# Layer 2 of a fused four-layer graph network: one 512-column moving operand, edge counts on ScalarE, another sequence

## The chip, the cores and the metric

One core of a Trainium2 chip runs one kernel launch that computes all four layers for all 16 graphs. The metric is the device time of that launch in microseconds. An engine is named as in the profile: PE is TensorE (its matmuls; PEld are its weight loads), DVE is VectorE, ACT is ScalarE, POOL is GpSimd, SP is SyncE, which here only issues transfers.

## The reference

Each of 16 graphs has 1024 nodes with 256 features and a symmetric 0/1 adjacency with self-loops. Every layer is x = x + f(relu(layernorm(x)), adj). Layers 0 and 1 are single-head attention layers, layer 3 is a four-head attention layer with a layer norm of its own, and layer 2, which the change is about, is a mean over neighbours:

```python
def _L2_gnn_ref(x, adj, W_msg, W_upd, bias):
    a = adj.astype(x.dtype)
    h = jnp.einsum('bnf,fu->bnu', x, W_msg)
    msg_sum = jnp.einsum('bij,biu->bju', a, h)
    deg = jnp.sum(a, axis=1)
    messages = jnp.where(deg[..., None] > 0, msg_sum / jnp.maximum(deg, 1.0)[..., None], 0.0)
    out = jnp.einsum('bnf,fu->bnu', x, W_upd) + messages + bias
    return jax.nn.relu(out)
...
x = x + _L0_gnn_ref(h, adj, L0_gnn_W, L0_gnn_a)      # attention over axis 1, elu
x = x + _L1_gnn_ref(h, adj, L1_gnn_W, L1_gnn_a)      # attention over the last axis, elu
x = x + _L2_gnn_ref(h, adj, L2_gnn_W_msg, L2_gnn_W_upd, L2_gnn_bias)
x = x + _L3_gnn_ref(h, adj, L3_gnn_W, ...)           # 4 heads of 64
```

## The kernel before

Nodes lie on the 128 partitions, eight tiles of 128 nodes to a graph. `graph(b)` writes out the four layers of graph b as a generator that yields now and then; a loop at the end of `tile_simple_stack` interleaves the generators of neighbouring graphs by the numbers they yield, so that the first layer of graph b+1 lies beside the last ones of graph b. That gives a rank to each instruction. The class `Order` then schedules everything anew: it walks through time with a planned cost for each instruction (`costs`), takes on each engine the ready instruction of the lowest rank, and fixes the order that comes out by dependencies. `STAY` says how far in rank it may deviate in order to stay in layer 3's half-array matmuls (128x64 weights, line 1238) or out of them, because PE pays for the change between the two kinds. So each number in a `yield`, in `STAY`, `APART`, `LEAD` or `SHIFT` moves instructions on all engines.

The matmuls are in fp32, except in layer 2. There, line 1154 projects a node tile with the message weights into PSUM. ScalarE writes the scaled result twice: `hi` in fp32r, a shorter format (line 1156), and `rest` in fp32 (line 1158); DVE stores the difference as `lo`, also fp32r (line 1159). `hi` and `lo` are the two parts of the messages. The 0/1 adjacency comes as eight column blocks of 512 KB through POOL's queue (`load_adj`, line 828), four buffers in turn. For each block j of 128 receiving nodes, PE multiplies the block with the eight tiles of `hi` and then with the eight tiles of `lo`, 258 columns each (line 1170), into the bank that already holds the update projection (line 1164). Columns 256 and 257 of `hi` are 1 and 0, so that column 256 of the sum counts the edges; `lo` has zeros there. ScalarE scales the result into `v` (line 1178) and copies the count into `edges` (line 1179), DVE adds the bias (line 1180), and `residual` adds the result to x and begins the next layer's norm. The PSUM pool `hd_ps` (two banks) holds the results of layer 2 and of layer 3's heads.

Elsewhere: line 936 are the projections of all layers, 930 the transposes of the normed input, 1040 and 1102 the products of layers 0 and 1 with their weights `p`, which DVE makes (lines 1048, 1050 and 1109); line 1225 makes the weights of a head of layer 3, and line 1246 is ScalarE's copy of a head's result out of PSUM. `Mask.step` (line 820) turns the adjacency into bytes and sums the edges by ScalarE. `tail` is the norm at the end of layer 3. At the very end DVE compares the edges of `squares` with those of `edges`, and a flag decides whether a slower general version runs after it.

Of the kernel before, what the change touches and what calls it, by code (L numbers as in the profile page):

```python
# [9 lines left out]
F32 = mybir.dt.float32  # L10
# [5 lines left out]
P = 128  # L16
# [405 lines left out]
class Order:  # L422
# [7 lines left out]
    STAY = {False: 31470.0, True: 35569.0}  # L430
# [33 lines left out]
    def costs(self, k):  # L464
# [182 lines left out]
def tile_simple_stack(  # L647
# [46 lines left out]
    unread = const.tile([P, D], U8)  # L694
    ones = const.tile([P, P], F32)
# [136 lines left out]
    def inv_std(var, n, scale, eps):  # L832

        rs = tile_of(small, [P, NT * H], F32, tag="rstd", name="rs", bufs=6)
# [7 lines left out]
    class Norm:  # L842
# [22 lines left out]
        def pair(self, xs, g, sums=None):  # L865
# [16 lines left out]
            if sums is not None:  # L882
                for k in range(2):
                    nc.scalar.activation(  # L884
                        unread, xs[:, 2 * g + k, :], AF.Square, bias=shift[:, k : k + 1], accum_out=self.var[:, 2 * g + k : 2 * g + k + 1]
# [78 lines left out]
    class Row:  # L964
# [5 lines left out]
        def add(self, n, f):  # L970
# [3 lines left out]
            nc.tensor.matmul(self.ps[g][:, k * P : (k + 1) * P], ones, diag, start=True, stop=True)  # L974
# [36 lines left out]
    def layer0(b, xs, m, norm, after):  # L1011
# [8 lines left out]
        for n in range(NT):  # L1020
# [5 lines left out]
            yield 3.85  # L1026
# [5 lines left out]
        yield 5.25  # L1032
# [11 lines left out]
        for j in range(NT):  # L1044
# [14 lines left out]
            yield 2.21  # L1059
        for i, ps in enumerate(early):  # L1060
            product(ps, i, NT - 1)
        for i in range(NT):
# [11 lines left out]
            yield 3.49  # L1074


    def layer1(b, xs, mask, norm, after):
        hs = new_hs()
        by_pe = Row() if b == 0 else None
        for n in range(NT):  # L1080
# [4 lines left out]
            yield 0.77  # L1085
# [9 lines left out]
        yield 2.71  # L1095
# [10 lines left out]
        for j in range(NT):  # L1106
# [6 lines left out]
            yield 3.18  # L1113
        for i in range(NT):
# [14 lines left out]
            yield 4.42  # L1129
# [9 lines left out]
    def layer2(b, xs, norm, after):  # L1139
# [8 lines left out]
        hi = tile_of(state, [P, NT, W3], F32R, tag="hs", name="hi", bufs=3)  # L1148
        lo = tile_of(state, [P, NT, W3], F32R, tag="hs", name="lo", bufs=3)
        nc.vector.memset(hi[:, :, D : D + 1].bitcast(F32), 1.0)  # L1150
        nc.vector.memset(hi[:, :, D + 1 : D + 2].bitcast(F32), 0.0)
        nc.vector.memset(lo[:, :, D : D + 2].bitcast(F32), 0.0)
        for n in range(NT):
            ps = project(norm, wx[2], n, D)
            by = z[:, n : n + 1]
            nc.scalar.activation(hi[:, n, :D], ps[:, :D], AF.Copy, scale=by)  # L1156
            rest = tile_of(work, [P, D], F32, tag="e", name="rest", bufs=2)
            nc.scalar.activation(rest, ps[:, :D], AF.Copy, scale=by)
            nc.vector.tensor_tensor(lo[:, n, :D], rest, hi[:, n, :D].bitcast(F32), op=OP.subtract)
            yield 0.91  # L1160
        for j in range(NT):
# [6 lines left out]
            for h in (hi, lo):  # L1168
                for i in range(NT):
                    nc.tensor.matmul(  # L1170
                        ps[:, : D + 2], adj_n[j][:, i, :], h[:, i, : D + 2],
                        start=False, stop=(h is lo and i == NT - 1), skip_group_check=True,
                    )
            k = b * NT + j
            if j + 4 < NE:
# [3 lines left out]
            nc.scalar.copy(edges[:, k : k + 1], ps[:, D : D + 1])  # L1179
            nc.vector.tensor_tensor(v, v, rows["bias2"], op=OP.add)  # L1180
            residual(xs, j, v, after)
            yield 1.61


    def layer3(b, xs, mask, norm, res):
# [6 lines left out]
        for n in range(NT):  # L1192
# [12 lines left out]
            yield 1.07  # L1205
# [11 lines left out]
        yield 3.57  # L1217
        for h in range(H):
            next_row = everywhere(d_row[h + 1], "row3") if h + 1 < H else None
            pss = [tile_of(hd_ps, [P, HALF], F32, tag="hd", name="ps_o3", bufs=2) for _ in range(NHALF)]  # L1220
            for j in range(0, NT, run):
# [21 lines left out]
                yield 1.17 * run  # L1243
# [6 lines left out]
    def tail(b, xs, hs, res):  # L1250
# [4 lines left out]
        for g in range(NHALF):  # L1255
# [7 lines left out]
            yield 20.37  # L1263
            nc.vector.tensor_tensor(of, of, hs[:, t, :D].rearrange("p t (h e) -> p t h e", e=HO), op=OP.add)
            yield 4.99
            nc.vector.tensor_reduce(m[:, 0, :], o, axis=AX.X, op=OP.add)
            yield 3.22
            total = m[:, 0, :].unsqueeze(2).to_broadcast([P, PER * H, HO])
            nc.vector.scalar_tensor_tensor(o, total, -1.0 / HO, o, op0=OP.mult, op1=OP.add)
            yield 8.10  # L1270
# [8 lines left out]
        for t, o, of, m, sq in halves:  # L1279
            nc.vector.tensor_reduce(m[:, 1, :], sq, axis=AX.X, op=OP.add)  # L1280
            rs.append(inv_std(m[:, 1, :], PER * H, 1.0 / HO, 1e-6))
            yield 1.47
        for g, (t, o, of, m, sq) in enumerate(halves):
            r = rs[g][:, : PER * H].unsqueeze(2).to_broadcast([P, PER * H, HO])
            if g == 0:

                nc.vector.tensor_tensor(of, of, along("gamma3"), op=OP.mult)
                yield 10.12
                of1 = halves[1][2]
                nc.vector.tensor_tensor(of1, of1, along("gamma3"), op=OP.mult)  # L1290
                yield 0.66
            nc.vector.tensor_tensor(o, o, r, op=OP.mult)
            yield 0.00
            if b < B - 1:
                nc.vector.tensor_tensor(of, of, along("beta3"), op=OP.add)
            yield 5.43
# [4 lines left out]
            yield 0.82  # L1301

    def graph(b):
# [5 lines left out]
        for g in range(NT // 2):  # L1309
            norm.pair(xs, g)  # L1310
            m.step()
            yield 2.74
        for layer, inputs in ((layer0, (m,)), (layer1, (m.bytes,)), (layer2, ())):
            yield 1.81
# [5 lines left out]
        yield 1.19  # L1320
# [7 lines left out]
    def loads(b):  # L1328
        loaded[b] = load_x(b)
        yield 17.93  # L1330
        masks[b] = Mask(b)
        yield 0.17


    APART, LEAD = 129.59, 35.70
    SHIFT = {0: 3.07, 1: 1.51, 2: 0.13, 13: -0.44, 14: -0.27, 15: -0.26}
    def more():

        weights01(1, w1, w1_t, a1, (1, 0))
        yield 89.77  # L1340
        weights2()
        yield 0.34
        weights3()
        yield 27.01
# [6 lines left out]
    queue = [(58, 0, more())] + [(begins[b], b, graph(b)) for b in range(B)] + [(begins[b] - LEAD, b, loads(b)) for b in range(1, B)]  # L1351
# [10 lines left out]
    bad = tile_of(small, [P, 4], F32, tag="bad", name="bad", bufs=4)  # L1362
# [79 lines left out]
```

## Time and profile before

| | |
|---|---|
| time, median of 3 runs | 2426.45 us (2425.6 to 2430.18) |
| the profiled execution's own time | 2429.41 us |
| its span | 2428.0 us |
| mean granted TensorE clock | 0.991 |
| instructions | 63180, of which 26244 matmuls and as many weight loads |

The span is the stretch from the first to the last recorded instruction, and the execution's time is 1.4 us longer. In the profile, "mean ns" of a matmul is the time in the pipeline of one, from its start to its modelled end. Matmuls overlap, so the rate at which PE takes them is read from the chain of work, where a row gives the stretch of time that so many of them fill one after the other. An fp32 matmul of the program appears as two in the trace, an fp32r matmul and a transpose as one.

### The profile page before, as it was taken

To read this page: it belongs to the slowest core of one execution; us is meant where nothing else is said; L and a number is where in the kernel's file an instruction comes from. 1 tells how busy PE (TensorE), PEld (TensorE's weight loads), DVE (VectorE), ACT (ScalarE), POOL (GpSimd) and SP (SyncE) were. 2 spreads that over 40 slices of the span, in tenths; PEclk is the share of its full clock that TensorE was granted. 3 is DMA by queue.
4 is the path that set the end of the run, shared out by engine and by line. 5 is a ranking of instruction groups with operands and counts; after the bars stand their busy time and mean duration, and the time that the engine had idled before them with its cause. 6 is when DMAs were issued, how large, how long until landed. Compare 5 with 4: busy or idle time off the path is not lost.

```text
span 2428.0 us, 63180 instructions
## 1 busy us (share of the span) xinstructions
PE 2361.5 (97%) x26244; PEld 2106.7 (87%) x26244; DVE 1964.4 (81%) x3871; ACT 1455.2 (60%) x4062; POOL 469.3 (19%) x454
## 2 busy tenths in 40 slices
PE   7999999999999999999999999999999999999984
PEld 5889888988888889888998989889888998989874
DVE  6478697996979888787897969879787896978867
ACT  5765657567475665757567475665757566475340
POOL 1120310303113031220303113031220303103021
PEclk9999999999999999999999999999999999999997
DMA  5452342624344263342624334263342634244021
GB/s 177 88 110 89 70 97 87 140 85 92 94 105 101 84 126 98 79 97 78 142 93 92 93 101 106 84 119 101 84 97 75 144 93 92 89 104 89 19 63 37
DMA packets 212008, 231.65 MB, mean 95 GB/s; under 512 B 10328, under 2 KB 160960, under 8 KB 211712
## 3 DMA queue, kind: packets, MB, share of 16 engines
q0 software_dynamic: 137728, 83.90, 19.5%
q1 hardware_dynamic: 73984, 143.62, 18.9%
q8 instruction: 208, 3.41, 0.6%
q14 instruction: 88, 0.72, 0.1%
HBM read 210.25 MB, written 17.22 MB: 94 GB/s over the span
## 4 chain that ended last, share of the span: by engine, by line
PE 86%; DMA 5%; ACT 4%; DVE 3%; POOL 1%; issue 1%; SPq 0%; ACTq 0%; DVEq 0%
PE ps_o L1238 18%; PE ps_o L1040 17%; PE ps_proj L936 17%; PE ps_o L1102 16%; PE ps_o L1170 10%; PE ps_o L1164 4%; PE pt_h L930 4%; DMA raw<-in_adj_t 4%; ACT mask L820 1%; DVE p L1225 1%; POOL rs L836 1%; ACT hn L911 1%; ACT hi L1156 1%; DMA d_row<-e_row 0%; DMA row<-d_row 0%
## 5 line engine op out<-in xcount | busy, mean ns | idle before, releaser
L1225 DVE SCALAR_TENSOR_TENSOR p<-row,q,mask 128x1024 f32<-128x1024 f32 x512 | 617.9, 1279 | 63.0 <-PE ps_o L1238 58.6
L936 PE MATMUL ps_proj<-wx,ht 128*128 128x258 f32 (+2 forms) x2048 | 514.3, 387 | 6.7 <-ACT hs L1194 3.9
L1238 PEld LDWEIGHTS ps_o<-hb,p 128*64 128x64 f32 x16384 | 488.1, 138 | 27.8 <-issue 20.6
L1238 PE MATMUL ps_o<-hb,p 128*64 128x65 f32 x16384 | 502.2, 223 | 4.7 <-DVE p L1225 2.3
L1040 PE MATMUL ps_o<-hs,p 128*128 128x256 f32 x2048 | 477.8, 381 | 4.3 <-ACT hs L1052 4.3
L1102 PE MATMUL ps_o<-hs,p 128*128 128x257 f32 x2048 | 468.8, 382 | 3.9 <-ACT v L1127 2.2
L1102 PEld LDWEIGHTS ps_o<-hs,p 128*128 128x128 f32 x2048 | 381.5, 190 | 61.4 <-ACT v L1127 6.9
L936 PEld LDWEIGHTS ps_proj<-wx,ht 128*128 128x128 f32 x2048 | 371.7, 191 | 67.6 <-ACT hs L1082 6.5
L1040 PEld LDWEIGHTS ps_o<-hs,p 128*128 128x128 f32 x2048 | 381.1, 191 | 54.8 <-ACT hs L1052 4.7
L835 POOL TENSOR_SCALAR rs<-mv 128x4 f32<-128x4 f32 (+1 forms) x112 | 44.9, 401 | 1317.6 <-ACT unread L884 1298.9
L836 POOL TENSOR_TENSOR rs<-rs,neg_half 128x4 f32<-128x4 f32 (+2 forms) x144 | 265.9, 1846 | 12.0
L911 ACT ACTIVATE hn<-xs,shift 128x256 f32<-128x256 f32 x384 | 177.1, 504 | 77.3 <-PE pt_h L930 43.0
L1170 PE MATMUL ps_o<-hi,adj 128*128 128x258 f32 x1024 | 202.3, 320 | 2.1 <-ACT hi L1156 1.0
L1246 ACT ACTIVATE res<-ps_o 128x260 f32<-128x260 f32 x128 | 49.8, 389 | 254.2 <-PE ps_o L1238 253.9
L820 ACT ACTIVATE mask<-raw 128x512 uint8<-128x512 int32 x248 | 156.1, 632 | 53.6 <-DMA raw<-in_adj_t 52.7
L930 PE MATMUL pt_h<-ident,hn 128*128 128x128 f32 x1024 | 175.8, 278 | 2.0 <-ACT hn L911 1.8
L1006 DVE SCALAR_TENSOR_TENSOR xs<-v,xs 128x256 f32<-128x256 f32 x384 | 160.3, 418 | 17.8 <-ACT v L1127 11.2
L828 POOL DMA_DIRECT2D adj<-in_adj x128 | 114.8, 899 | 293.9 <-PE ps_o L1170 292.3
L1170 PEld LDWEIGHTS ps_o<-hi,adj 128*128 128x128 f32 x1024 | 150.1, 190 | 14.9 <-ACT hi L1156 5.4
L1048 DVE SCALAR_TENSOR_TENSOR p<-row,q 128x1024 f32<-128x1024 f32 x128 | 161.4, 1271 | 1.8 <-ACT row L980 1.6
L930 PEld LDWEIGHTS pt_h<-ident,hn 128*128 128x128 f32 x1024 | 126.0, 141 | 36.5 <-ACT hn L911 10.3
L931 ACT COPY ht<-pt_h 128x512 f32<-128x512 f32 x256 | 147.1, 575 | 16.8 <-PE pt_h L930 14.0
(124 smaller groups left out, 3009.0 us busy)
## 6 DMA issues: line engine op xcount, KB each, us to landing
raw<-in_adj_t SPq DMA_DIRECT2D x256, 256.0 KB
adj<-in_adj POOLq DMA_DIRECT2D x128, 512.0 KB, 5.3
row<-d_row SPq DMA_DIRECT2D x108, 512.0 KB
xs<-in_x POOLq DMA_DIRECT2D x32, 512.0 KB, 4.4
out<-xs SPq DMA_DIRECT2D x32, 512.0 KB
wx<-in_w SPq DMA_DIRECT2D x3, 256.0 KB
d_row<-e_row SPq DMA_DIRECT2D x45, 4.0 KB
wts<-in_w_t SPq DMA_DIRECT2D x2, 256.0 KB
```

Of the source, the lines that this page charges most:

```text
L820: nc.scalar.activation(to, raw, AF.Square, accum_out=total)
L836: nc.gpsimd.tensor_tensor(rs[:, :n], rs[:, :n], neg_half[:, :n], op=OP.pow)
L911: nc.scalar.activation(hn, xs[:, 2 * g + k, :], AF.Relu, scale=scale, bias=bias)
L930: nc.tensor.transpose(pt[:, c, k * P : (k + 1) * P], hn[:, c * P : (c + 1) * P], ident)
L936: nc.tensor.matmul(ps[:, :width], norm.ht[:, c, n * P : (n + 1) * P], w[:, c, :width], start=(c == 0), stop=(c == DC - 1))
L1006: nc.vector.scalar_tensor_tensor(x, v, 0.0, x, op0=OP.max, op1=OP.add, accum_out=after.sums[:, i % 2 : i % 2 + 1])
L1040: nc.tensor.matmul(ps[:, :D], ps_[j][:, i * P : (i + 1) * P], hs[:, j, :D], start=(j == 0), stop=(j == NT - 1))
L1048: nc.vector.scalar_tensor_tensor(p, row_a, q[:, j : j + 1], row_b, op0=OP.mult, op1=OP.max)
L1102: nc.tensor.matmul(ps[:, : D + 1], ps_[j][:, i * P : (i + 1) * P], hs[:, j, : D + 1], start=(j == 0), stop=(j == NT - 1))
L1170: nc.tensor.matmul(ps[:, : D + 2], adj_n[j][:, i, :], h[:, i, : D + 2], start=False, stop=(h is lo and i == NT - 1), skip_group_check=True,)
L1225: nc.vector.scalar_tensor_tensor(p, row, q[:, jj, h : h + 1], mask[:, jj, :], op0=OP.max, op1=OP.mult)
L1238: nc.tensor.matmul(pss[g][part, k * HW : (k + 1) * HW], ps_[t][:, i * P : (i + 1) * P][:, part], hbv[:, j + t, h, :], start=(j == 0 and t ...
```

## The change

In layer 2, `hi` and `lo` of a node tile lie side by side in one tile of 512 columns, and PE multiplies an adjacency tile with both at once, into the whole bank: eight matmuls of 512 columns for each block j instead of sixteen of 258. The two parts are no longer summed by the accumulation in PSUM: ScalarE scales the left half as before, and a new DVE instruction scales the right half and adds it. The column of ones is gone, and with it ScalarE's small copy; instead ScalarE reads each adjacency block (1024 numbers to a partition) in a copy that nobody reads and takes its sum. The sums now go by rows rather than by columns of the adjacency, so the comparison at the end is made on the totals of each graph. Three small memsets to a graph go. The planned cost of an fp32r matmul gets a term for its size. All numbers that lay the sequence are new, so the schedule as a whole is another one.

```diff
-    STAY = {False: 31470.0, True: 35569.0}
+    STAY = {False: 70844.0, True: 16885.0}
...
             if any("float32r" in a[3] for a in acc):
-                return 121.0, 330.0
+                t = max(121.0, 3.0 + size[0] / 2.4)
+                return t, t + 210.0
...
-    unread = const.tile([P, D], U8)
-    ones = const.tile([P, P], F32)
+    unread = const.tile([P, N], U8)
+    ones = const.tile([P, 1], F32)
...
-        hi = tile_of(state, [P, NT, W3], F32R, tag="hs", name="hi", bufs=3)
-        lo = tile_of(state, [P, NT, W3], F32R, tag="hs", name="lo", bufs=3)
-        nc.vector.memset(hi[:, :, D : D + 1].bitcast(F32), 1.0)
-        nc.vector.memset(hi[:, :, D + 1 : D + 2].bitcast(F32), 0.0)
-        nc.vector.memset(lo[:, :, D : D + 2].bitcast(F32), 0.0)
+        both = [tile_of(state, [P, NT, W3], F32R, tag="hs", name="hl", bufs=3) for _ in range(NHALF)]
+        hl = []
         for n in range(NT):
+            g, k = divmod(n, PER)
+            hl.append(both[g].rearrange("p n d -> p (n d)")[:, k * HALF : (k + 1) * HALF])
+            hi, lo = hl[n][:, :D], hl[n][:, D:]
             ps = project(norm, wx[2], n, D)
             by = z[:, n : n + 1]
-            nc.scalar.activation(hi[:, n, :D], ps[:, :D], AF.Copy, scale=by)
+            nc.scalar.activation(hi, ps[:, :D], AF.Copy, scale=by)
             rest = tile_of(work, [P, D], F32, tag="e", name="rest", bufs=2)
             nc.scalar.activation(rest, ps[:, :D], AF.Copy, scale=by)
-            nc.vector.tensor_tensor(lo[:, n, :D], rest, hi[:, n, :D].bitcast(F32), op=OP.subtract)
-            yield 0.91
+            nc.vector.tensor_tensor(lo, rest, hi.bitcast(F32), op=OP.subtract)
+            yield 0.77
...
-            for h in (hi, lo):
-                for i in range(NT):
-                    nc.tensor.matmul(
-                        ps[:, : D + 2], adj_n[j][:, i, :], h[:, i, : D + 2],
-                        start=False, stop=(h is lo and i == NT - 1), skip_group_check=True,
-                    )
+            for i in range(NT):
+                nc.tensor.matmul(ps, adj_n[j][:, i, :], hl[i], start=False, stop=(i == NT - 1), skip_group_check=True)
             k = b * NT + j
+            nc.scalar.activation(
+                unread, adj_n[j].rearrange("p i c -> p (i c)").bitcast(F32), AF.Copy, accum_out=edges[:, k : k + 1]
+            )
             if j + 4 < NE:
                 adj_n.append(load_adj(b, j + 4))
             v = tile_of(work, [P, D], F32, tag="v", name="v", bufs=2)
             nc.scalar.activation(v, ps[:, :D], AF.Copy, scale=z[:, j : j + 1])
-            nc.scalar.copy(edges[:, k : k + 1], ps[:, D : D + 1])
+            nc.vector.scalar_tensor_tensor(v, ps[:, D:], z[:, j : j + 1], v, op0=OP.mult, op1=OP.add)
             nc.vector.tensor_tensor(v, v, rows["bias2"], op=OP.add)
             residual(xs, j, v, after)
-            yield 1.61
+            yield 1.94
...
-                yield 1.17 * run
+                yield 2.07 * run
...
-    APART, LEAD = 129.59, 35.70
+    APART, LEAD = 146.48, 41.63
...
-    nc.vector.tensor_tensor(t, t, edges, op=OP.not_equal)
-    nc.vector.tensor_reduce(bad[:, 0:1], t, axis=AX.X, op=OP.add)
-    nc.vector.tensor_scalar(t, edges, 0.0, None, op0=OP.is_le)
+    t_0 = tile_of(work, [P, D], F32, tag="v", name="t_0", bufs=2)[:, : B * NT]
+    nc.vector.tensor_scalar(t_0, t, 0.0, None, op0=OP.is_le)
+    nc.vector.tensor_reduce(bad[:, 0:1], t_0, axis=AX.X, op=OP.add)
+    nc.vector.tensor_tensor(t, t, edges, op=OP.subtract)
+    nc.vector.tensor_reduce(bad[:, 3:], t.rearrange("p (b n) -> p b n", b=B), axis=AX.X, op=OP.add)
...
```

The other yields, `SHIFT`, and the sizes of a few small tiles change as well.

More of the change, by code (lines that the diff above doesn't have):

```diff
@@ L973, in add @@
             nc.vector.tensor_scalar(diag, ident, f, None, op0=OP.mult)
[L974 removed]
+            nc.tensor.matmul(self.ps[g][:, k * P : (k + 1) * P], ones.to_broadcast([P, P]), diag, start=True, stop=True)
         def rows(self, scales, tag="row"):
@@ L1350, in tile_simple_stack @@
     begins = [b * APART + SHIFT.get(b, 0.0) for b in range(B)]
-    queue = [(58, 0, more())] + [(begins[b], b, graph(b)) for b in range(B)] + [(begins[b] - LEAD, b, loads(b)) for b in range(1, B)]
+    queue = [(106.61, 0, more())] + [(begins[b], b, graph(b)) for b in range(B)] + [(begins[b] - LEAD, b, loads(b)) for b in range(1, B)]
     while queue:
```

78 lines of the change are left out of this document (39 added, 39 removed).

## The prediction

> **What bounds the kernel now.** I read the page's totals first, then the steady stretch by windows, then the chain in order of time, then the groups and waits of layer 2.
>
> ```profile
> span 2428.0 us, 63180 instructions
> PE 2361.5 (97%) x26244; PEld 2106.7 (87%) x26244; DVE 1964.4 (81%) x3871; ACT 1455.2 (60%) x4062; POOL 469.3 (19%) x454
> ```
> PE is busy nearly always. As its ends are modelled, that alone does not make it the bound, so I look at stretches: one whole steady graph (1044 to 1190), its layer 2 (1141.7 to 1178), and the end.
>
> ```profile
> 1044.00:1190.00 146.00, 145.65 (x1637) 130.73 (x1636) 121.56 (x238) 90.98 (x255) 29.39 (x28) 1.00 0.40 99
> 1141.70:1178.00 36.30, 36.21 (x233) 33.16 (x232) 25.27 (x64) 25.63 (x74) 13.58 (x13) 1.00 0.53 110
> 1164.00:1178.00 14.00, 14.00 (x99) 13.31 (x98) 13.91 (x34) 8.65 (x25) 9.00 (x8) 1.00 0.43 79
> 2320.00:2428.00 108.00, 67.77 (x1220) 61.24 (x1218) 82.07 (x115) 24.41 (x70) 26.06 (x16) 0.83 0.23 56
> ```
> The columns are the stretch, its length, busy PE, PEld, DVE, ACT and POOL, then clock, DMA share and GB/s. In a steady graph PE leaves 0.35 us of 146; DVE has 24 us and ACT 55 us left. In layer 2's second part DVE is nearly full too (13.91 of 14). At the end, where no next graph fills the holes, PE is not the bound.
>
> ```profile
> 148.38 1.92 PE ps_o L1170 x16
> 133.68 1.96 PE ps_o L1170 x16
> 165.47 1.73 PE ps_o L1040 x8
> 387.41 17.60 PE ps_o L1102 x80
> 2139.50 17.60 PE ps_o L1102 x80
> ```
> These rows of the chain (start, us, what) give rates: 16 fp32r matmuls of 258 columns fill 1.92 to 1.96 us, 120 to 122.5 ns each; eight fp32 ones of 256 columns 1.73 us, 216 ns each. The last two rows show the period: the same piece of layer 1 recurs twelve graphs later, so (2139.50 - 387.41) / 12 = 146.0 us for a graph. Period times number of graphs is what the kernel's time is made of, and the period is PE's work.
>
> **The change part by part. Matmuls.** A graph has 8 x 16 = 128 matmuls of 258 columns, 128 x 0.121 = 15.5 us. It gets 64 of 512. No row shows an fp32r matmul of 512 columns. The dear end is growth in proportion: 0.121 x 512 / 258 = 240 ns, 15.4 us for 64, a gain of 0.1 us. For the cheap end I take the half-array rows of layer 3, where 256 matmuls of 65 columns fill 7.62 us, two at a time: 59.5 ns for a pair. From there to 216 ns at 256 columns an fp32 column costs 0.82 ns and the fixed part is 6 ns. An fp32 matmul of 256 columns thus occupies PE as long as 512 fp32r columns at half that price would: 0.41 x 512 + 6 = 216 ns. By the same formula 258 columns would cost 112 ns; the 8 to 10 ns above it look like something that a short matmul does not cover, such as its weight load, and in the rows of 216 ns a weight load of the same 128 columns is covered. I take 216 ns, as the row of L1040 is nearest: it has the same weights and the same time at PE. That makes 64 x 0.216 = 13.8 us, a gain of 1.7 us for a graph; if the 8 ns stay, 64 x 0.224 = 14.3, a gain of 1.2. Over 16 graphs: 27 us, with 19 and 2 as the worse ends.
>
> [...]
>
> **ScalarE.** Eight sums of 1024 elements a graph. The nearest rows are a Square of the same width and a read of the accumulator, and what goes is the small copy:
>
> ```profile
> L1272 ACT ACTIVATE sq<-res 128x1024 f32<-128x1024 f32 x32 | 34.2, 1068 | 13.9 <-DVE res L1269 13.9
> L884 ACT ACTIVATION_READ_ACCUMULATOR unread<-xs,shift 128x1 f32 x256 | 48.4, 189 | 0.0
> L1179 ACT COPY edges<-ps_o 128x1 f32<-128x1 f32 x128 | 19.1, 149 | 0.0
> L1180 DVE TENSOR_TENSOR v<-v,row_bias 128x256 f32<-128x256 f32 x128 | 54.2, 423 | 34.6 <-ACT v L1178 33.7 <-ACT edges L1179 0.8
> ```
> That is at most 8 x (1.068 + 0.189 - 0.149) = 8.9 us. The steady graph has 55 us left, so on the whole ACT goes to about 100 of 144. In layer 2 it is tight: 25.6 + 8.9 = 34.5 us, where PE needs 36.3 - 1.7 = 34.6. But a sum needs only the landed block, not the matmuls. In the changed kernel's order of instructions two of the eight sums stand ahead of the first `v`, the others alternate with `v`, and PE's order mixes more of the next graph's layer 0 (L1040) into layer 2, which widens that stretch. A sum ahead of `v` makes it up to 1.1 us later; the two banks of `hd_ps` give PE a block of about 2.6 us (8 x 0.216 + 4 x 0.216) of cover. I cost it at nothing, and at up to 1 us a graph if the cover fails.
>
> **DVE.** Eight more instructions of 256 elements (row of L1180) less three memsets of 0.07 us: 8 x 0.423 - 0.2 = 3.2 us a graph, 121.6 to 124.8 of 144. `v` is 0.42 us later for its followers, hidden by the same second bank. The first block now waits for both parts of a node tile, so DVE's subtraction (L1159) stands ahead of it, where `hi` sufficed before; the new order puts L1040 matmuls there. Cost nothing, at worst 0.4 us a graph. [...]
>
> **Adjacency blocks.** POOL may now fetch block j+4 only after the sum of block j too.
>
> ```profile
> POOL adj L828 <- PE ps_o L1170: 292.3, 65, 11.4
> adj<-in_adj POOLq DMA_DIRECT2D x128, 512.0 KB, 5.3
> ```
> POOL already waits for PE's last reader there, and what is queued behind it are the norm's small instructions. A block takes 0.9 us to issue and 5.3 to land. By the new order some 10 us of PE's work lie between the last matmul of block j and the first of block j+4, so a sum that ends 2 us late is covered. Cost nothing.
>
> **The sequence.** PE changes between the two kinds of matmul 150 times in both orders, so nothing is won there. Between stalls that the chain shows as pieces of ACT and odd 0.1 us gaps, a steady graph loses about 1.5 us now. A new order can save that or double it: -1.5 to +1.5 us a graph; I take 0. At the end, layer 2 of the last graph is still PE's (blocks 3.0 us apart, falling to 2.8), and the new DVE order puts the former graph's last steps (L1292 to L1299, 1.2 us each) ahead of it instead of inside: I credit 1 us; one sum ahead of the last projections takes it back. The final comparison gets one more small DVE instruction, while PE still works.
>
> **Sum.** 16 x 1.7 = 27 us of PE's work, of which I give back 2 for stalls in layer 2: the profiled 2429.4 would become 2404.4. It lay 3.0 us above the median of the runs, so against 2426.45 I forecast 2402 us, a period of about 144.4.
>
> **The rivals.** (1) Slower: ACT becomes the bound of layer 2. Its queue is in order; if four of the eight sums each hold back a `v` that PE needs a bank of, by 1.07 us, a graph loses 4.3 us and gains 1.7: +2.6 x 16 = 42 us, 2468. It decides from 1.7 us of stall a graph. For it: 34.5 against 34.6 us above. Against: sums that may run early, and the wider stretch. (2) The change does not speed up PE: 512 columns cost 240 ns. Then 2 us are won: 2424, no difference. For it: 120 ns where the formula says 112. Against: the 216 ns of L1040. (3) The new order also takes the present stalls out: 1 us more a graph, 2386. For it: 1.5 us are there. Against: PE's busy time leaves 0.35 us, and stalls before a first fp32r matmul will remain.
>
> **How the numbers follow.** Forecast 0.72, with an own range of 2394 to 2412 (19 to 27 us of matmuls, 0.5 us of stalls a graph either way). Rival 1 0.08, most of it near +0 to +20 us; rival 2 0.10, half of it faster by an order that stalls less; rival 3 0.10. A measurement tells about 0.2%, 5 us, from no change. Faster: 0.72 + 0.10 + 0.05 + 0.01 = 0.88; same: 0.05 + 0.01 = 0.06; slower 0.06. The range of 2388 to 2417 takes in the forecast's own, most of rival 3 and the milder stalls, and leaves out about 0.17.
>
> **What would show it.** Right: the matmul row of layer 2 counts 1024, eight of them fill 1.73 us of chain, the pieces of L1102 recur every 144 to 145 us, PE leaves under 1 us in a steady graph. Wrong: eight fill 1.9 us (rival 2); PE waiting for ACT's `v` or DVE's new line before L1164, with ACT busy over 95% of layer 2 (rival 1); waits of PE for adjacency blocks; a period that falls by less than the matmuls do.

## The result, and the profile after

| | before | after |
|---|---|---|
| time, median (lowest to highest) | 2426.02 us (2423.5 to 2430.18), 4 runs | 2447.73 us (2445.75 to 2449.48), 4 runs |
| profiled execution, its span | 2429.41, 2428.0 us | 2449.48, 2447.7 us |
| mean granted clock | 0.991 | 0.993 |

The ratio is 1.009 (95% interval 1.0079 to 1.0102): the kernel became 21.7 us slower, where 24 us less were forecast. First the totals of the page after the change.

```profile
span 2447.7 us, 61454 instructions
PE 2363.0 (97%) x25220; PEld 2040.4 (83%) x25220; DVE 2013.8 (82%) x3952; ACT 1568.8 (64%) x4190; POOL 464.2 (19%) x454
```
1024 matmuls are gone, and PE is busy 1.5 us longer than before. DVE has 49 us more and ACT 114, where the sum had 16 x 3.2 = 51 and at most 16 x 8.9 = 142.

The windows of a steady graph and of the worst one (columns as before: PE, PEld, DVE, ACT, POOL, clock, DMA share, GB/s):

```profile
1044.00:1190.00 146.00, 144.31 (x1567) 125.23 (x1566) 123.15 (x238) 96.85 (x260) 27.48 (x29) 1.00 0.42 99
452.00:598.00 146.00, 141.67 (x1549) 121.63 (x1548) 122.02 (x231) 93.33 (x254) 27.59 (x27) 1.00 0.37 96
```
PE left 0.35 us of 146 before in the first of these stretches and 1.2 in the second; now it leaves 1.7 and 4.3. The granted clock is the full one in both, so PE waits for something. The chain of work gives the rate of the new matmul, and the groups give the new instructions:

```profile
2204.24 1.85 PE ps_o L1170 x8
2216.85 1.86 PE ps_o L1170 x8
```
```profile
L1170 PE MATMUL ps_o<-hl,adj 128*128 128x512 f32 x1024 | 310.0, 429 | 8.3 <-DVE hl L1160 8.3
L1172 ACT ACTIVATE unread<-adj 128x1024 uint8<-128x1024 f32 x128 | 135.1, 1055 | 0.3
L1179 DVE SCALAR_TENSOR_TENSOR v<-ps_o,z,v 128x256 f32<-128x256 f32 x128 | 61.0, 481 | 97.6 <-ACT v L1178 97.2
```
Eight matmuls of 512 columns fill 1.85 us, 231 ns each: 1.73 us was to show the forecast right and 1.9 us rival 2. PE also idles 8.3 us in all for `hl`, the tile with both parts, which DVE's subtraction completes.

The start of the first matmul of layer 2 in a graph, taken from the traces, shows where the time goes:

| graph | before, us | after, us | after minus before |
|---|---|---|---|
| 1st | 121.5 | 123.6 | 2.1 |
| 3rd | 413.3 | 417.2 | 3.9 |
| 5th | 706.4 | 718.9 | 12.5 |
| 6th | 852.4 | 865.5 | 13.1 |
| 16th | 2309.1 | 2330.4 | 21.3 |
| end of the span | 2428.0 | 2447.7 | 19.7 |

The start costs 2 us, the 3rd and 4th graph 8.6, the ten steady graphs at the end 8.2, the others 2.4. (The start says little: in later runs with the changed kernel's order it lies between 121.3 and 128.7 us.) In the steady ones the period is (2330.4 - 865.5) / 10 = 146.5 us, against 145.7 before. The end gave back 1.6 us; 1 was credited.

In the 3rd and 4th graph PE is idle for 8.0 of 302 us (417 to 719), before for 1.7 of 293. The timeline shows a dozen waits there for different things; only one, 0.68 us, is for `hl`. The four longest:

```profile
424.91 1.92 PE L931 MATMUL pt_h<-ident,hn 128*128 128x128 f32 x8 [1.24 <-ACT hn L912]
466.94 2.05 PE L937 MATMUL ps_proj<-wx,ht 128*128 128x264 f32 x8 [0.85 <-ACT hs L1194]
533.48 1.13 PE L1103 MATMUL ps_o<-hs,p 128*128 128x257 f32 x4 [1.25 <-DVE p L1110]
636.02 0.44 PE L931 MATMUL pt_h<-ident,hn 128*128 128x128 f32 x2 [1.01 <-ACT hn L912]
```

**One steady graph from near.** Layer 2 needs the norm of layer 1's output: ACT's row sums (L885), a power on POOL (L837), DVE's scales (L902, L903), ACT's normed rows (`hn`, L912), PE's transposes of them (L931), ACT's copy (`ht`, L932), PE's projections (L937). The timeline of PE there (start, us, line, in brackets the idle time ahead and its releaser), then those of DVE and POOL:

```profile
1162.58 1.89 PE L1041 MATMUL ps_o<-hs,p 128*128 128x256 f32 x8
1165.22 0.73 PE L1170 MATMUL ps_o<-hl,adj 128*128 128x512 f32 x2 [0.75 <-DVE hl L1160]
1165.93 1.91 PE L931 MATMUL pt_h<-ident,hn 128*128 128x128 f32 x8
```
```profile
1162.49 1.28 DVE L1049 SCALAR_TENSOR_TENSOR p<-row,q 128x1024 f32<-128x1024 f32 x1
1164.67 0.16 DVE L902 TENSOR_TENSOR scales<-rs,deg 128x4 f32<-128x4 f32 x1 [0.90 <-POOL rs L837]
1164.75 0.42 DVE L1160 TENSOR_TENSOR hl<-rest,hl 128x256 fp32r<-128x256 f32 x1
```
```profile
1162.70 1.94 POOL L837 TENSOR_TENSOR rs<-rs,neg_half 128x4 f32<-128x4 f32 x1
```
POOL's power takes 1.94 us. DVE's scales wait 0.90 us for it; the subtraction L1160, queued behind them, is late, and PE waits 0.75 us for it. Then the transposes come at ACT's pace (four rows of `hn` in 2.08 us): eight fill 1.91 us, where six in a row filled 0.82 us a little earlier. That is about 1.8 us of PE in one graph (0.75, and 1.91 less eight times the 0.11 us, 109 ns in the trace, from one transpose to the next in a row). In the kernel before, POOL's row at the same step of its norm is

```profile
1143.86 1.01 POOL L836 TENSOR_TENSOR rs<-rs,neg_half 128x4 f32<-128x4 f32 x1
```
and these windows show the surroundings of the two norms, before's first:

```profile
1140.00:1156.00 16.00, 15.91 (x88) 13.63 (x87) 5.05 (x18) 12.87 (x35) 1.20 (x2) 1.00 0.19 61
```
```profile
1155.00:1171.00 16.00, 15.05 (x68) 11.74 (x67) 14.98 (x31) 13.24 (x33) 2.21 (x2) 1.00 0.00 1
```
The old sequence had this norm in a stretch where DVE was busy for 5.05 of 16 us, while PE filled its time with the projections of the next graph's layer 0. The new one has it beside the weights of that layer, with DVE busy for 14.98 of 16 us. PE's filling there is L1041, which needs DVE's products `p`.

The wait for POOL at the scales, from the views of L837 and of before's L836 (total us, times):

```profile
  DVE scales L902: 15.7, 18
```
```profile
  DVE scales L901: 5.0, 15
```

### The profile page after: what moved, and what is told of

Its sections match the earlier page's. It is cut to its first block, busy times and chain, and to the rows that moved or that the text cites. A ratio compares the mean times of both kernels' runs of the same rounds, so it can differ in the third digit from the quotient of the medians.

```text
span 2447.7 us, 61454 instructions
## 1 busy us (share of the span) xinstructions
PE 2363.0 (97%) x25220; PEld 2040.4 (83%) x25220; DVE 2013.8 (82%) x3952; ACT 1568.8 (64%) x4190; POOL 464.2 (19%) x454
## 5 line engine op out<-in xcount | busy, mean ns | idle before, releaser
L937 PE MATMUL ps_proj<-wx,ht 128*128 128x258 f32 (+2 forms) x2048 | 507.0, 385 | 5.2 <-ACT hs L1194 2.2
L1041 PE MATMUL ps_o<-hs,p 128*128 128x256 f32 x2048 | 479.1, 381 | 6.1 <-ACT hs L1053 5.1
L1103 PE MATMUL ps_o<-hs,p 128*128 128x257 f32 x2048 | 477.5, 382 | 4.3 <-DVE p L1110 2.4
L1041 PEld LDWEIGHTS ps_o<-hs,p 128*128 128x128 f32 x2048 | 384.7, 191 | 63.0 <-ACT hs L1053 8.3
L937 PEld LDWEIGHTS ps_proj<-wx,ht 128*128 128x128 f32 x2048 | 374.5, 190 | 70.8 <-ACT ht L932 4.8
L836 POOL TENSOR_SCALAR rs<-mv 128x4 f32<-128x4 f32 (+1 forms) x112 | 50.4, 450 | 1536.8 <-ACT unread L885 1200.9
L1170 PE MATMUL ps_o<-hl,adj 128*128 128x512 f32 x1024 | 310.0, 429 | 8.3 <-DVE hl L1160 8.3
L837 POOL TENSOR_TENSOR rs<-rs,neg_half 128x4 f32<-128x4 f32 (+2 forms) x144 | 252.4, 1753 | 12.0
L912 ACT ACTIVATE hn<-xs,shift 128x256 f32<-128x256 f32 x384 | 178.6, 501 | 79.4 <-DVE shift L880 46.2
L1170 PEld LDWEIGHTS ps_o<-hl,adj 128*128 128x128 f32 x1024 | 189.3, 189 | 47.6 <-DVE hl L1160 13.7
L1006 DVE SCALAR_TENSOR_TENSOR xs<-e,xs 128x256 f32<-128x256 f32 x256 | 105.9, 421 | 102.9 <-ACT e L1071 77.3
L931 PE MATMUL pt_h<-ident,hn 128*128 128x128 f32 x1024 | 178.8, 279 | 8.0 <-ACT hn L912 5.8
L931 PEld LDWEIGHTS pt_h<-ident,hn 128*128 128x128 f32 x1024 | 126.0, 141 | 57.8 <-ACT hn L912 27.9
L932 ACT COPY ht<-pt_h 128x512 f32<-128x512 f32 x256 | 147.0, 575 | 39.2 <-PE pt_h L931 38.0
```

The costliest lines, as they stand in the source:

```text
L912: nc.scalar.activation(hn, xs[:, 2 * g + k, :], AF.Relu, scale=scale, bias=bias)
L931: nc.tensor.transpose(pt[:, c, k * P : (k + 1) * P], hn[:, c * P : (c + 1) * P], ident)
L932: nc.scalar.copy(self.ht[:, :, g * 2 * P : (g + 1) * 2 * P], pt)
L937: nc.tensor.matmul(ps[:, :width], norm.ht[:, c, n * P : (n + 1) * P], w[:, c, :width], start=(c == 0), stop=(c == DC - 1))
L1041: nc.tensor.matmul(ps[:, :D], ps_[j][:, i * P : (i + 1) * P], hs[:, j, :D], start=(j == 0), stop=(j == NT - 1))
L1103: nc.tensor.matmul(ps[:, : D + 1], ps_[j][:, i * P : (i + 1) * P], hs[:, j, : D + 1], start=(j == 0), stop=(j == NT - 1))
```

## The experiments

Three questions: operations or sequence; what each operation is worth when the order on every engine is kept; and what in the new sequence holds PE.

**Operations or sequence.** *e1_old_seq*: the changed operations with all the numbers of the sequence from the kernel before.

```diff
-    STAY = {False: 70844.0, True: 16885.0}
+    STAY = {False: 31470.0, True: 35569.0}
... all yields, APART, LEAD, SHIFT likewise
```


> The changed operations (512 columns, sums by ScalarE, DVE's addition) under the numbers that lay the sequence before (yields, STAY, APART, LEAD, SHIFT); the planned cost of an fp32r matmul stays as changed. Theory S (the new numbers make the stalls; the operations gain PE the 16 x (128 x 0.121 - 64 x 0.232) = 10 us that the traces show): 2415 to 2424 us, PE's stalls in a steady graph back at about 1.7 us. Theory O (the operations make the stalls in any sequence: the sums stand ahead of work that PE waits for, the first block waits for both parts): 2440 us or more, with PE waiting for DVE's L1160 and for hn of L912 as in the changed kernel.

*e2_new_seq*: the operations of the kernel before with the new numbers, the same diff the other way.

> The kernel before with the new numbers of the sequence and nothing else. Theory S: it takes on the stalls, +15 to +25 us, 2440 to 2452 us. Theory O: the numbers are harmless, 2422 to 2432 us.

*e3_no_sums*: the changed kernel without ACT's edge sums.

```diff
-            nc.scalar.activation(
-                unread, adj_n[j].rearrange("p i c -> p (i c)").bitcast(F32), AF.Copy, accum_out=edges[:, k : k + 1]
-            )
```


> The changed kernel without ScalarE's sums over the adjacency blocks (leaves out that part of the final comparison; the output is the reference's). The schedule is made anew for what is left. Theory O, if the sums are what hurts: 8.4 us of ACT a graph and the later fetch of the blocks go, and the time falls by 10 to 20 us, to 2428 to 2438. Theory S: under 5 us either way, 2443 to 2452.

*e4_256_sums*: as e1, but two matmuls of 256 columns summed in PSUM, no DVE addition, ACT's sums kept.

```diff
+            for part in range(2):
+                for i in range(NT):
+                    nc.tensor.matmul(ps[:, :D], adj_n[j][:, i, :], hl[i][:, part * D : (part + 1) * D], ...)
-            nc.vector.scalar_tensor_tensor(v, ps[:, D:], z[:, j : j + 1], v, op0=OP.mult, op1=OP.add)
```


> As e1 (old numbers), but the two parts are multiplied one after the other, 256 columns each, into the same half of the bank, so that PSUM adds them and DVE's addition goes; ScalarE's sums stay. Gives the price of 256 columns: if the 8 to 10 ns above 0.41 x columns + 6 are the weight load's, 256 columns cost 120 ns as 258 do; if a column costs 0.437 ns and the fixed part is 7 ns (the line through 258 and 512 columns), 119 ns. Either way PE gains under 3 us in all over before. Theory S: 2420 to 2428 us. Theory O with the sums to blame: 2436 or more; O with the wide matmul's dependencies to blame: as S.

| run | us | ratio to before, 95% |
|---|---|---|
| e1_old_seq | 2513.27 | 1.0364 (1.0347 to 1.0381) |
| e2_new_seq | 2536.69 | 1.0457 (1.0440 to 1.0475) |
| e3_no_sums | 2508.10 | 1.0336 (1.0318 to 1.0353) |
| e4_256_sums | 2459.99 | 1.0137 (1.0119 to 1.0154) |

All four are slower than both kernels, three of them by over 2.4%, even e3, which only leaves work out. PE's busy time in a steady stretch of e1:

```profile
1044.00:1190.00 146.00, 141.47 (x1552) 122.60 (x1551) 122.49 (x236) 94.63 (x256) 30.27 (x28) 1.00 0.38 91
```
4.5 us of idle time in 146. By its number e1 falls under theory O, and e2 goes far beyond S; but e3, which takes the sums away, gains nothing of what O asked. Only e4's question on the price has an answer: in its trace 256 columns take 120 ns, as 258 do. So these runs cannot tell what an operation is worth: the scheduler makes another order as soon as a cost or a dependency changes, and here no set of numbers did well with a program that it was not laid for. From here on the order was kept, or the numbers were searched anew.

*e5_new_ops_searched* and *e6_old_ops_searched*: the operations of the changed kernel, and as a control those of the kernel before, each with numbers found by the same search, which used the durations in the traces.

```diff
-    STAY = {False: 70844.0, True: 16885.0}
+    STAY = {False: 84247.27, True: 100754.03}
-            yield 5.29
+            yield 5.93
-    APART, LEAD = 146.48, 41.63
+    APART, LEAD = 146.72, 67.37
... most other yields by a little
```


> The changed operations with other numbers for the sequence, found by trying some thousand sets against the durations that the traces show (512 columns at 231 ns, a pair of half-array matmuls at 59.5 ns, POOL's powers). Theory S (the sequence, not the operations, is the loss; the operations gain PE about 10 us): at least 15 us below the changed kernel, 2415 to 2432. Theory O: 2440 or more, since the operations carry their waits into any order.

> The control: the kernel before with numbers found by a search of the same kind and length. It shows what a search gives without the change: 2418 to 2428. If e5 is below it by more than 5 us, the operations are a gain; if the two are within 5 us, they are worth nothing here; if e5 is above by more, they cost.

e5 took 2432.06 us, ratio 1.0018 (1.0009 to 1.0027); e6 2442.38 us, ratio 1.0066 (1.0052 to 1.0079). With the same operations and other numbers, (1.0090 - 1.0018) x 2426 = 17.5 us of the 21.7 are gone, give or take 3.5; the same search made the old operations 16 us slower. Other numbers alone move the time by that much, in either direction. e5's windows of the two stretches:

```profile
1044.00:1190.00 146.00, 145.11 (x1572) 126.71 (x1571) 124.33 (x240) 97.01 (x263) 30.06 (x29) 1.00 0.40 99
452.00:598.00 146.00, 145.50 (x1574) 126.88 (x1574) 124.91 (x240) 99.42 (x264) 29.58 (x29) 1.00 0.41 98
```
PE leaves 0.9 and 0.5 us, where the changed kernel leaves 1.7 and 4.3. Cut at the starts of layer 2, the profiled executions show where e5 is faster:

| stretch, us | before | after | e5 |
|---|---|---|---|
| up to the 1st graph's layer 2 | 121.5 | 123.6 | 120.4 |
| 3rd and 4th graph | 293.1 | 301.7 | 292.3 |
| ten steady graphs | 1456.7 | 1464.9 | 1461.3 |
| the rest | 556.7 | 557.5 | 554.8 |

Half of the 18.9 us between the last two columns lies in the 3rd and 4th graph, and 3.6 in the steady ones. The norm ahead of layer 2 is not what sets these two sequences apart: e5 has POOL's power of 1.94 us there too, and a wait of PE of 0.69 us for `hl`, eight transposes in 1.91 us, and 9.2 us of waits for `hl` in all, against 8.3 in the changed kernel. The kernel before has none of the three at this step, and its steady graphs are the shortest.

**What the operations are worth at a fixed order.** In the next four kernels every engine does its instructions in the changed kernel's order; the schedule is laid with the costs planned for that kernel, and the traces show the same order.

*f1_480*:

```diff
-                nc.tensor.matmul(ps, adj_n[j][:, i, :], hl[i], ...)
+                nc.tensor.matmul(ps[:, :480], adj_n[j][:, i, :], hl[i][:, :480], ...)
-            nc.vector.scalar_tensor_tensor(v, ps[:, D:], z[:, j : j + 1], v, ...)
+            nc.vector.scalar_tensor_tensor(v[:, :224], ps[:, D:480], z[:, j : j + 1], v[:, :224], ...)
```


> The changed kernel with its very order of instructions on every engine, but layer 2's matmuls take 480 of the 512 columns (leaves out 32 columns of the second part, DVE adds 224 columns). By the line through 258 and 512 columns (0.437 ns a column, 7 ns fixed) one costs 217 ns, what the forecast took for 512. Theory R (the matmul's 231 instead of 216 ns is on the path): 1024 x 15 = 15 us less than the changed kernel, 2432. Theory L (what counts is where the order makes PE wait, and PE takes up the slack by waiting longer): under 5 us less, 2443 or more.

```profile
2206.86 1.74 PE ps_o L1170 x8
2212.51 1.73 PE ps_o L1170 x8
```
480 columns take 217 ns, 1 ns more than was forecast for 512. The time is 2442.05 us, ratio 1.0046 (1.0029 to 1.0063): 0.44%, 11 us less for 1024 x 14 ns = 14 us of matmul, and a little less DVE. With the intervals of both ratios it is 11 give or take 5 us, so most of what is saved here reaches the end. (The profiled execution was the slowest of its four, 2450.8 us; only its rate is used.)

*h3_two_256*: each wide matmul as two of 256 columns into the halves of the bank.

```diff
-                nc.tensor.matmul(ps, adj_n[j][:, i, :], hl[i], ...)
+                nc.tensor.matmul(ps[:, D:], adj_n[j][:, i, :], hl[i][:, D:], ...)
+                nc.tensor.matmul(ps[:, :D], adj_n[j][:, i, :], hl[i][:, :D], ...)
```


> The changed kernel with its order on every engine kept, but each matmul of 512 columns in layer 2 is made by two of 256 into the two halves of the bank, the half with lo first, so that both still need the whole of a node tile. It tells what one wide operand is worth at a fixed order. By the measured rates, 231 ns for 512 columns and 120 ns for 256, PE gets 1024 x (240 - 231) = 9 us more work. Theory M (the wide operand saves these 9 us and two thirds of a matmul's time lie on the path, as in the run with 480 columns): 2452 to 2457 us, so that without the new order the operations would have gained 5 to 9 us, and the order lost about 27. Theory P (in the mixed stream the wide operand is worth nothing): within 2 us of the changed kernel, 2446 to 2450 us. If it is over 2460 us, weight loads that the wide matmul halves were worth more than the rates say.

2454.16 us, ratio 1.0096 (1.0078 to 1.0113), 0.0006 above the changed kernel, or 1.5 us; the span of its profiled execution is 6.6 us longer (2454.3). By the rates PE got 1024 x (240 - 231) = 9 us more work. The intervals allow anything from nothing to 7 us, so they do not part the two theories: the wide operand is worth at most that much of the 27 us forecast.

*g1_64w*, run once: seven of eight weight loads halved to 64 columns.

```diff
-                nc.tensor.matmul(ps, adj_n[j][:, i, :], hl[i], ...)
+                part = slice(0, P if i == 0 else 64)
+                nc.tensor.matmul(ps[part, :], adj_n[j][:, i, part], hl[i], ...)
```


> The changed kernel with its very order, but seven of the eight matmuls of a block load only 64 columns of weights (leaves out half of the messages' rows). Asked is only the rate of 512-column matmuls in a run: if the 15 ns above 216 come from the weight load beside the stream, they fall to 216 to 224 ns; if they are the stream's own, they stay at 231 ns.

```profile
L1171 PEld LDWEIGHTS ps_o<-hl,adj 128*64 128x64 f32 x896 | 119.3, 135 | 77.6 <-DVE hl L1160 14.2
```
A weight load fell from 189 to 135 ns, and in runs of eight and more the matmul still took 230 ns; all 1024 of them kept PE busy for 309.1 us, against 310.0 in the changed kernel. So the load does not set the rate; the 231 ns go with the width of the moving operand. The one time, 2456.25 us, shows no gain.

*f2_small_sums*: the edge sums read 8 numbers instead of 1024.

```diff
-                unread, adj_n[j].rearrange("p i c -> p (i c)").bitcast(F32), AF.Copy, ...
+                unread[:, :8], adj_n[j].rearrange("p i c -> p (i c)").bitcast(F32)[:, :8], AF.Copy, ...
```


> The changed kernel with its very order, but ScalarE's sums over the adjacency blocks read 8 instead of 1024 numbers (leaves out the comparison of the edges), so each takes about 0.25 instead of 1.1 us in its old place in the queue. Theory A (ScalarE is late in layer 2 because of the sums, and PE's waits for transposes and for the two parts come from that): PE's 1 to 2 us of waits around the first block go, 15 to 25 us less, 2423 to 2433. Theory L (the waits come from other neighbours in the order: POOL's norm and DVE behind it): under 6 us less, 2441 to 2448.

2449.59 us, ratio 1.0077 (1.006 to 1.0095): 0.0013 or 3 us under the changed kernel, give or take 5. That is theory L, and fits the prediction's cost for the sums: nothing, and at most 1 us a graph.

**What holds PE in the new sequence.** Again the changed kernel's order, with single places moved in the norm between layers 1 and 2.

*h1_swap*: L1160 goes ahead of the scales L902 that wait for POOL, in 12 graphs.

```diff
+            if a == "scales" and b == "hl" and line[i] not in self.before[line[i + 1]]:
+                line[i], line[i + 1] = line[i + 1], line[i]
```


> The changed kernel with one edit of DVE's order: in the twelve graphs where the small `scales` multiplication (L902), which waits for POOL's norm, stands ahead of a subtraction that completes a node tile of the moving operand (L1160), the two change places; all other engines keep their order. Theory S (PE's wait of 0.9 us a graph before the third block of columns comes from that place in the order): the wait goes, 12 x 0.9 = 11 us less, 2437 us; if PE then waits as long for the transposes that hang on the same POOL result, 3 us less or nothing. Theory O (the two parts are simply complete too late): no change, 2447.

2447.54 us, ratio 1.0092 (1.0076 to 1.0109). PE's waits for `hl` fell from 8.3 to 0.5 us in all, and as much turned up ahead of the transposes, which wait for `hn`.

*h2_quiet_norm*: L1049 moved behind the scales, so that POOL's power has no long product beside it, and an edge sum moved behind L912.

```diff
+            line[i:end] = line[i + 1 : end] + line[i : i + 1]     # DVE: L1049 behind L903
+            line[i : i + 5] = line[i + 1 : i + 5] + line[i : i + 1]     # ACT: L1172 behind four L912
```


> The changed kernel in its own order, except for two moves in the norm between layers 1 and 2 of a graph. On DVE the product L1049 (1.28 us) that stood ahead of the scales L902 stands behind L903 (12 graphs); on ACT the second of two edge sums L1172 (1.06 us) stands behind the four L912 (13 graphs). PE, POOL and the transfers keep their order. In the changed kernel POOL's power L837 of this norm took 1.94 us, beside an L1049 that was running when it began; in the kernel before the same power took 1.01 us beside no such product, and DVE waited 15.7 us in all for it against 5.0. Theory N (the sequence put this norm beside DVE's long products, so that the power, then DVE's scales, ACT's L912 and PE's transposes are late): the power goes to 1.0 us, DVE's wait at L902 falls to about 5 us, PE's waits of 0.75 to 0.9 us before L1170 and of 0.2 us between the transposes shrink, and the time falls by 0.8 to 1.3 us in each of 12 graphs, to 2432 to 2438 us. Theory A (PE is held by something else and only meets the wait here; the product that is moved makes the next L1041 late instead): 2445 to 2449 us, with new waits of PE at L1041 or L937.

```profile
1171.73 1.01 POOL L837 TENSOR_TENSOR rs<-rs,neg_half 128x4 f32<-128x4 f32 x1
1172.77 0.16 DVE L902 TENSOR_TENSOR scales<-rs,deg 128x4 f32<-128x4 f32 x1 [1.17 <-POOL rs L837]
1175.36 1.04 ACT L1172 ACTIVATE unread<-adj 128x1024 uint8<-128x1024 f32 x1
1177.02 1.99 PE L937 MATMUL ps_proj<-wx,ht 128*128 128x256 f32 x8 [1.07 <-ACT ht L932]
```
2458.59 us, ratio 1.0110 (1.0089 to 1.0131): no gain. The power did fall from 1.94 to 1.01 us, and PE no longer waited for `hl`. But the moved sum stood ahead of L932, and PE waited 1.07 us there.

*h4_quiet_norm_2*: the same, with the sum moved on to a gap of ACT.

```diff
-            line[i : i + 5] = line[i + 1 : i + 5] + line[i : i + 1]
+            while not (name(line[end])[0] == "v" and "z2" in name(line[end])):
+                end += 1
+            line[i:end] = line[i + 1 : end] + line[i : i + 1]
```


> As h2_quiet_norm (DVE's product L1049 behind the scales of the norm between layers 1 and 2 in 12 graphs), but the second edge sum goes farther back on ACT, ahead of the first v (L1178) of layer 2, where ACT was idle for 1 us. In h2_quiet_norm POOL's power there fell from 1.94 to 1.01 us and ACT's L912 began 0.94 us sooner after the last row sum, but the moved sum held back the copy L932 by 1.04 us, and PE waited there. Theory N (this norm, late by DVE's product and by the sum, is what PE waits for): PE's waits there fall by 0.8 to 1.0 us in 12 graphs, the time lies 8 to 13 us under the changed kernel, 2435 to 2440 us (ratio 1.004 to 1.006). Theory A (PE's wait only turns up at the next place): 2445 to 2460 us, ratio over 1.008.

```profile
1163.51 0.73 PE L1170 MATMUL ps_o<-hl,adj 128*128 128x512 f32 x2
1171.18 1.19 PE L1170 MATMUL ps_o<-hl,adj 128*128 128x512 f32 x4 [0.55 <-DVE hl L1160]
```
2455.2 us, ratio 1.0109 (1.0094 to 1.0125). The first wait was gone. But 8 us later PE waited for further rows of `hl`, which now stood behind the moved product. DVE had lost time: it waited 1.17 us for POOL and did the 1.28 us product afterwards, 2.45 us, where product and wait had taken 1.28 + 0.90 = 2.18.

*h5_quiet_searched*: both moves of h4 in e5.

> The same two moves in the kernel with the searched numbers (2432 us, ratio 1.0018), whose norm between layers 1 and 2 has the same power of 1.94 us and the same wait of PE for hl (0.7 us) and between the transposes. Theory N: 8 to 13 us less, 2419 to 2424 us, ratio 0.997 to 0.9985: faster than both kernels. Theory A: 2428 to 2440 us, ratio over 1.000.

2438.65 us, ratio 1.0039 (1.0025 to 1.0053), worse than e5. Theory N, a late norm that such a move mends, failed in both sequences.

*k1_half_mask* and *k2_half_mask_before*: less work for DVE in this stretch, in the new order and in the old.

```diff
-            nc.vector.scalar_tensor_tensor(p, row_a, q[:, j : j + 1], row_b, op0=OP.mult, op1=OP.max)
+            nc.vector.scalar_tensor_tensor(p, row_a, q[:, j : j + 1], row_b, op0=OP.mult, op1=OP.min)
...
-            nc.vector.scalar_tensor_tensor(p, p, 1.0, mask[:, j, :], op0=OP.mult, op1=OP.mult, accum_out=z[:, 0:1])
+            nc.vector.scalar_tensor_tensor(p[:, :HALF], p[:, :HALF], 1.0, mask[:, j, :HALF], op0=OP.mult, op1=OP.max, accum_out=z[:, 0:1])
```


> The changed kernel with its order on every engine kept; DVE's step that puts the mask on the weights of layer 0 (L1051, 1.22 us, 8 in a graph) covers 512 of 1024 columns. The weights are left unmasked: L1051 takes the greater of weight and mask, and L1049 the smaller of its two products, at the same sizes of operands otherwise. DVE gets 8 x 0.6 = 4.8 us less to do in a graph, all of it in or near the stretch from layer 1's end into layer 2, where it is busy for 14.98 of 16 us. Theory D (the new sequence put the norm between layers 1 and 2 beside DVE's products, and DVE's pace binds PE there): PE's waits for hl and hn shrink from about 2.0 to under 1 us a graph, and the time falls by 12 to 25 us, to 2423 to 2436 us. Theory C (the chain of the norm itself binds, power, scales, L912, transposes, whatever DVE does beside it): within 5 us of the changed kernel, 2443 to 2450 us.

> The control: the kernel before in its own order, with the same step of DVE (line 1050) cut to 512 columns in the same way. There the norm between layers 1 and 2 lies in a stretch in which DVE is busy for 5.05 of 16 us. Theory D: little to win, 2420 to 2428 us. If it gains as much as k1_half_mask does, DVE's pace binds both sequences alike, and D does not tell where the change lost its time.

```profile
1160.46 0.73 PE L1170 MATMUL ps_o<-hl,adj 128*128 128x512 f32 x2 [0.42 <-DVE hl L1160]
1161.17 1.91 PE L931 MATMUL pt_h<-ident,hn 128*128 128x128 f32 x8
```
k1: 2442.98 us, ratio 1.0059 (1.0046 to 1.0073); k2: 2428.8 us, ratio 0.9994 (0.9986 to 1.0003). The same relief of DVE is worth 0.31%, 7.5 us give or take 4, in the new order and nothing measurable in the old one. So DVE's load costs time in the new order and not in the old one. That it does so at this norm is read from the traces: in the graph shown the wait for `hl` shrank from 0.75 to 0.42 us, and the ten steady graphs took 1461.7 instead of 1464.9 us. But 7.5 us lie between the two theories. The transposes still take 1.91 us, the 3rd and 4th graph still 301.1 us, and what holds the rest was not shown.

## Why the prediction was wrong, point by point

- **Matmuls, failed: the term was mis-sized.** 216 ns were taken from an fp32 matmul of 256 columns, with 0.41 ns for an fp32r column and 6 ns fixed. An fp32r matmul of 512 columns takes 231 ns, also with a weight load of half the width; 217 ns is the price of 480. The prediction had the sign of it, 120 ns for 258 columns where its formula gave 112, but took the 8 ns for a fixed cost such as an uncovered weight load. They were a dearer column, 0.44 ns, and so became 15 ns at 512. By the rates the gain is 16 x (128 x 0.121 - 64 x 0.231) = 11 us instead of 27, and at a fixed order h3 allows nothing to 7. PE's busy time rose by 1.5 us where the sum needed it to fall by 27. The "dear end", growth in proportion, 240 ns and 2 us in all, was near; it got 0.10 as rival 2.
- **The sequence, failed: "I take 0".** It cost most of the loss: e5 has 17.5 us less with the same operations. The step's own range, +1.5 us a graph, would have allowed 24 us, but the range of the time took in only 0.5 us a graph, 8 us. Half of what e5 saves lies in the 3rd and 4th graph, where PE's waits are spread over many places; a steady graph showed DVE's load beside the norm ahead of layer 2. The prediction said that DVE is nearly full in layer 2 (13.91 of 14 us) and did not ask what the new order would lay beside it.
- **"At worst 0.4 us" for the first block, failed in size.** `hi` alone no longer suffices, and PE waits 0.75 us for `hl` in the graph shown. Yet h1 shows that this wait alone is not what costs: without it PE waits for `hn`.
- **ACT's sums, DVE's addition, adjacency blocks: right.** f2 puts the sums at 3 us, give or take 5. DVE's new row reads PSUM and takes 481 ns, 58 more than the 423 of L1180 before, by which it was priced: 0.5 us of DVE in a graph. POOL does wait for the sums before it fetches blocks (118.8 us in 33 waits), but no wait of PE for a block was found.
- **Rival 1** had the right sign by the wrong mechanism: ACT did not become the bound, it is idle for 49 us of a steady graph. The bound that the prediction named, PE, is still busy for 97%; what changed is that it waits more, 1.7 instead of 0.35 us in the steady stretch and 8.0 instead of 1.7 in the 3rd and 4th graph.
- **The sum of the failures.** The profiled execution was to take 2404.4 us and took 2449.5, 45 more. Of these 20 to 27 are matmul gain that is not there (16 by the rates alone), about 17.5 the sequence, measured against e5, and some 3 the sums, which is within the noise.

**What stays open.** That other numbers for the sequence give back 17.5 us is shown; which places of the sequence make up the loss is not. No move at the norm gave time back, and half the work of one DVE step gave back a third. The 8.6 us of the 3rd and 4th graph were not tested at all. That the norm's latency and the lack of other work for PE make up the rest of the steady graphs is argued from the timelines, not shown. Nor is it settled what the new operations are worth under the best sequence: e5 is 10 us under e6, but each search reached only one of many sequences. No kernel here beat the one before by more than the noise.

## What to carry to other kernels

Where a scheduler lays the order, a change of the operations is a change of the order, and the order may be worth more than the operations. Find first in which stretches the time was lost, and then look in the new order for what is laid beside each chain of small steps (norms, powers, transposes), and give a new sequence a cost of its own. Price a matmul by a row of its own type and width, or take the end that grows in proportion. Where a formula misses a row that is known, ask whether the miss grows with the size. To learn what an operation is worth, keep the order on every engine and change only the operation.

## What the runs showed of the hardware

- An fp32r matmul on 128 rows of weights takes 120 ns for 256 columns (e4, h3), 217 for 480 (f1) and 231 for 512 when it follows others of its kind, or about 0.44 ns a column and 7 ns. A weight load of 64 columns instead of 128 (135 instead of 189 ns) leaves the 512 columns at 230 ns (g1).
- A change of PE between whole-array matmuls and layer 3's half-array ones costs about 0.1 us each way; both kernels have 75 of them in either direction. In the kernel before, the first half-array matmul starts 308 to 311 ns after the start of the last one of L936 or L1040, where 216 to 222 ns pass at the median from one of these to the next; after a transpose it is 202 instead of 109 ns. On the way back the next matmul starts 152 ns after the last half-array one, where another pair of half-array matmuls would start after 52.
- POOL's power of four numbers to a partition takes 1.01 us, or 1.94 us if DVE has a product of 1024 columns (1.28 us) under way when it begins; when that product was moved away (h2), it took 1.01 us again. In the whole trace of the changed kernel, 28 of the 96 such powers begin beside a DVE instruction of 1024 columns and take 1.86 to 1.95 us; the other 68 take 1.01 to 1.35. The time is real, though spans on POOL are rough in a profile: in the graphs shown of both kernels DVE's scales, which wait for the power, begin 0.03 us after its recorded end. In k1 the addition ahead of the power met such a product instead, and took 0.90 us where it had taken 0.28. The price of one product of L1049 is thus 0.93 us in the graph shown; by what way DVE slows POOL was not shown.

```profile
1157.89 0.90 POOL L836 TENSOR_SCALAR rs<-mv 128x4 f32<-128x4 f32 x1 [15.81 <-ACT unread L885]
1158.87 1.01 POOL L837 TENSOR_TENSOR rs<-rs,neg_half 128x4 f32<-128x4 f32 x1
```
